# Row sums of attention: all four heads added at once on GpSimd, one key block left to the ones-matmuls, and new durations in the scheduler's model

## The chip, the cores and the metric

The kernel runs on one core of a Trainium2 chip. The metric is the device time of one execution in microseconds; lower is better. The engines are named as the profile names them: PE (TensorE, matmuls; PEld are its weight loads), DVE (VectorE), ACT (ScalarE), POOL (GpSimd) and SP (SyncE, whose queue issues the DMAs here).

## The reference

One transformer block on x of shape (2, 1024, 512): a modulated layer norm, causal attention with 32 query heads over 8 key/value heads of width 64 and rotary positions, a gated residual, a second modulated layer norm, and a feed-forward block with ternary weights. The part that matters here is attention's softmax:

```python
scores = jnp.einsum('bhqd,bhkd->bhqk', q, k) / jnp.sqrt(jnp.float32(D))
scores = jnp.where(causal[None, None], scores, jnp.finfo(x.dtype).min)
attn = jax.nn.softmax(scores, axis=-1)
out = jnp.einsum('bhqk,bhkd->bhqd', attn, v)
return out.transpose(0, 2, 1, 3).reshape(b, s, H * D) @ Wo
```

All of it is fp32. Every output row is divided by the sum of its exponentials over the keys: the row sum.

## The kernel before, in words

**Stages.** First come layer norm, the projections to q, k and v and the rotation (to about 340 us), written out in a fixed order. Then attention (about 340 to 1400 us) and the feed-forward (to the end), both put in order by a planner. The quantization of the feed-forward's weights (`ternary`, line 1074, 48 pieces) runs inside the attention stage.

**Units.** Attention works in 64 units (line 511): a batch, a group of four query heads that share a key head, and a block of 256 queries (i = 0 to 3). A unit has `nb = 2 * i + 2` key blocks of 128 keys: 2, 4, 6 or 8, in 16 units each. The last two blocks lie on the diagonal; in the very last one only 128 of the 256 queries count.

**Steps of a unit.** Before the scores, PE multiplies q with k once to get each row's maximum (`pm`); DVE reduces these from PSUM (`mx`), joins them (`mm`, line 771), and PE, ACT and a DMA turn them into one more row of the q tile, so that the scores come out with the maximum subtracted. For each key block j: two score matmul pairs (`score`, two heads each) into PSUM; two ACT exponentials (`expo`) into the tile `e` (four heads by 256 queries; 5 buffers); on the last two blocks a POOL select that zeroes the future (`causal`, line 827); and the value matmuls (`value`, line 833) in full fp32, which accumulate into `po`. The exponentials are also added over the key blocks into the tile `acc` (`total`, line 846): per block POOL adds heads 0 and 1 in one instruction and head 2 in another, DVE adds head 3. With two blocks only, ACT copies the half that has one addend (`first_total`). At the end of a unit four matmuls with a tile of ones, 32 columns wide, sum `acc` over the partitions, one head each, side by side in the array (`row_sum`, line 902). The result goes by ACT and DMAs through DRAM, is inverted, comes back as `ri`, and DVE multiplies the output with it (`normalize`); ACT and DVE split the product in a high and a low part, and six matmuls for each half project it (`project`), after which DVE adds it to the output rows `oacc`.

**What sets the order.** Every step is a task (`add`, line 70) with an engine, an assumed cost in us, a due time, the tasks it waits for, and the buffers it takes. `Plan.run` (line 90) plays the tasks through at these costs: each time it takes the engine that can start first, and there, among the tasks that could start, the one with the earliest due time, with an advance of 4 us for tasks of PE's present mode. Mode 1 is full fp32 (`value`, `row_sum`), mode 0 all the rest. The order in which tasks are taken is the program order of each engine; on the chip every engine works strictly in it and waits by semaphore. The costs come from small formulas: `pe`, `dv`, `po`, `ac` (lines 523 to 533). They decide the order only. PSUM has 3 score buffers, 4 buffers shared by `pm`, `pr`, `pj`, `pq` and others, and one for `po`. The queue of an engine is therefore a list fixed in advance; what is late in it holds all that stands behind it.

Of the kernel before, what the change touches and what calls it, by code (L numbers as in the profile page):

```python
# [58 lines left out]
class Plan:  # L59
# [30 lines left out]
    def run(self):  # L90
        wait, then, ready = {}, {}, {}
        for t in self.tasks:
            deps = {d.n: d for d in t.after + t.before}
            wait[t.n] = len(deps)
            for d in deps.values():
                then.setdefault(d.n, []).append(t)
            if not deps:
                ready.setdefault(t.eng, []).append((0.0, t))
        free, moving, ring, modes, left = {}, 0.0, 0.0, {}, len(self.tasks)
        while left:  # L100
            best = None
            for eng, ts in ready.items():
                opts = []
                for r, t in ts:
                    at = self.room(t)
                    if at is not None:
                        opts.append((max(r, at), t))
                if not opts:
                    continue
                start = max(free.get(eng, 0.0), min(o[0] for o in opts))  # L110
                if best is not None and start >= best[0]:
                    continue
                t = min((o for o in opts if o[0] <= start), key=lambda o: (o[1].due - STICK * (o[1].mode == modes.get(eng)), o[1].n))[1]
                best = (start, t)
            start, t = best
            left -= 1
            ready[t.eng] = [o for o in ready[t.eng] if o[1] is not t]
            for tag in t.takes:
                self.slots[self.alias.get(tag, tag)].append(lambda t=t, tag=tag: t.users[tag])
            t.emit()  # L120
            if t.eng == "T" and t.mode < modes.get("T", 0):
                start += 0.09
            modes[t.eng] = t.mode
            free[t.eng] = t.done = start + t.cost
            if t.eng is None:
                free[None] = t.done = 0.0
            if t.dma:
                ring = max(start + (0.26 if t.eng == "A" else 0.03), ring) + t.cost
                free[t.eng] = ring
                moving = max(ring + 0.7, moving) + t.dma / 360e3  # L130
                t.done = moving + 0.95
            for d in then.get(t.n, ()):
                wait[d.n] -= 1
                if not wait[d.n]:
                    r = max([a.done + (self.LAG if a.eng != d.eng or a.dma else 0.1) for a in d.after], default=0.0)
                    ready.setdefault(d.eng, []).append((r, d))
# [7 lines left out]
def block_kernel(ctx, tc, x, wq, wk, wv, wo, wgu, wpj, cin, wmod, cos, sin, out):  # L144
# [378 lines left out]
    def pe(n):  # L523
        return n / 2400 + 0.003

    def dv(n):
        return 0.069 + n / 960

    def po(n):
        return 0.05 + n * 0.0023  # L530

    def ac(n, psum=True):
        return (0.05 if psum else 0.094) + n / 1200

    KB = 1024
    add = plan.add
# [136 lines left out]
    def attention(u):  # L673
# [18 lines left out]
        if i == 0:  # L692
# [46 lines left out]
            lw = add("S", 0.46, t0 - 2, load_wo, order=(opened,), takes=("wos",), dma=512 * KB)  # L739
            wh = [add("A", ac(512, 0), t0 + 5 + 2 * c, lambda c=c: wo_hi(c), (lw,), takes=(("woH",), ())[c]) for c in range(2)]  # L740
            wh[1].order(wh[0])
            wl = [add("V", dv(512), t0 + 6 + 3 * c, lambda c=c: wo_lo(c), (wh[c],), takes=(("woL",), ())[c]) for c in range(2)]
            wl[1].order(wl[0])
            lw.hold("wos", *wh, *wl)
            wd["t"] = wh + wl
# [48 lines left out]
        for n, a in enumerate(jobs):  # L794
# [4 lines left out]
            m.hold("x", r)  # L799
            tops.append(m)  # L800
            reds.append(r)
        jn = add("V", 0.077, t0 - LEAD, top_join, reds, takes=("mm",))
        z.hold("mx", jn)
        tt = add("T", 0.11, t0 - LEAD, top_T, (jn,), takes=("x",))
        jn.hold("mm", tt)
# [37 lines left out]
            d["on"] = tp.tile([128, 512], F32, name="on", bufs=4)  # L843
            A.activation(d["on"].rearrange("p (a q) -> p a q", q=256), d["po"], AF.Copy)

        def total(j, eng, hs):
            q0 = 128 if j == nb - 1 else 0
            if "acc" not in d:
                d["acc"] = gp.tile([128, 4, 256], F32, name="acc", bufs=3)
            a = d["e", 0] if j == 1 else d["acc"]  # L850
            eng.tensor_tensor(d["acc"][:, hs, q0:], a[:, hs, q0:], d["e", j][:, hs, q0:], ALU.add)

        def first_total():
            d["acc"] = gp.tile([128, 4, 256], F32, name="acc", bufs=3)
            A.activation(d["acc"][:, :, 0:128], d["e", 0][:, :, 0:128], AF.Copy)

        ex, es, vals, sums, own = {}, {}, [], {}, None
        for j in range(nb):
            n = 128 if j == nb - 1 else 256
            due = due_s[(u, j)]  # L860
            es[j] = []
            for hp_ in range(2):
                p = add("T", 2 * pe(2 * n), due + 0.5 * hp_, lambda j=j, h=hp_: score(j, h),
                        [row, d["lq"][1], kd["one"]] + kd["l"] + d["lq"], takes=("s",))
                kd["use"].append(p)
                d.setdefault("sc", []).append(p)
                x_ = add("A", ac(2 * n), due + 0.5 + 0.5 * hp_, lambda j=j, h=hp_: expo(j, h), (p,), order=es[j],
                         takes=("e",) if hp_ == 0 else ())
                p.hold("s", x_)
                es[j].append(x_)  # L870
            ex[j] = es[j]
            if j >= nb - 2:
                ex[j] = [add("P", po(4 * 128) - 0.6, due - 1, lambda j=j: causal(j), es[j])]
            v = add("T", 2 * 4 * pe(n) + 0.05, due + 5, lambda j=j: value(j), ex[j] + [kd["lv"]], order=vals[-1:],
                    takes=("o",) if j == 0 else (), mode=1)
            kd["av"].append(v)
            vals.append(v)
            if j == 1 and nb == 2:
                own = add("A", ac(512, 0), due + 5, first_total, ex[0], order=(opened,), takes=("acc",))
            if j > 0:  # L880
                before = [own] if nb == 2 else sums[j - 1] if j > 1 else []
                q = []
                for a, z_ in ((0, 2), (2, 3)):
                    q.append(add("P", po((z_ - a) * n), due + 6, lambda j=j, a=a, z=z_: total(j, P, slice(a, z)), ex[j] + ex[0] + before,
                                 order=q[:1] or (opened,), takes=("acc",) if j == 1 and nb > 2 and not q else ()))
                if j == 1 and nb > 2:
                    own = q[0]
                q.append(add("V", dv(n), due + 6, lambda j=j: total(j, V, slice(3, 4)), ex[j] + ex[0] + before, order=(q[0],)))
                sums[j] = q
        for j in range(nb):  # L890
            users = [vals[j]] + (sums[j] if j else sums[1])
            if j == 0 and nb == 2:
                users.append(own)
            es[j][0].hold("e", *users)
        d["lq"][0].hold("t1", *tops, *d["sc"])
        d["lq"][1].hold("t2", *d["sc"])
        kd["use"].extend(tops)
# [3 lines left out]

        def row_sum():
            d["pr"] = xtile([128, 256], "pr")
            for h in range(4):
                T.matmul(d["pr"][h * 32:h * 32 + 32, :], ones, d["acc"][:, h, :], start=True, stop=True)

        def row_copy():
            d["ls"] = tp.tile([128, 256], F32, name="ls", bufs=1)
# [14 lines left out]
            for a in range(2):  # L923
                SY.dma_start(d["ri"][a * 64:a * 64 + 64, :], linv[u][a:a + 1, :].broadcast_to([64, 512]))

        rs = add("T", 4 * pe(256) + 0.15, t1_ + 4, row_sum, sums[nb - 1] + (sums[nb - 2] if nb > 2 else [own]), takes=("x*",), mode=1)
        own.hold("acc", rs)
        rc = add("A", ac(256), t1_ + 5, row_copy, (rs,), takes=("ls",))
        rs.hold("x*", rc)
        rt = add("S", 0.63, t1_ + 5, row_turn, (rc,), takes=("l8",), dma=16 * KB)  # L930
# [28 lines left out]
            else:  # L959
                V.tensor_tensor(acc, acc, d["pj", s], ALU.add)  # L960

        nm = add("V", dv(512), t1_ + 13, normalize, (gi, out_))
        gi.hold("ri", nm)
        hi_ = add("A", ac(512, 0), t1_ + 15, high, (nm,), takes=("oH",))
        lo_ = add("V", dv(512), t1_ + 17, low, (hi_,), takes=("oL",))
        out_.hold("on", hi_, lo_)
        pj = [add("T", 6 * pe(512), t1_ + 19 + s, lambda s=s: project(s), [hi_, lo_] + wd["t"], takes=("x*",)) for s in range(2)]
        hi_.hold("oH", *pj)
# [3 lines left out]
        for s in range(2):  # L972
# [1 line left out]
            sm.append(add(*(("A", ac(512)) if g == 0 else ("V", dv(512))), t1_ + 20 + s, lambda s=s: sum_up(s), [pj[s]] + prev_add.get(key, [])))  # L974
            pj[s].hold("x*", sm[s])
            prev_add[key] = [sm[s]]
        left_users.extend(tops + d["sc"] + vals + reds + [jn, tt, tc_, row] + sums[nb - 1] + sums[1] + ([own] if nb == 2 else []))
        outer_users.extend(())
        tail_users.extend(pj + sm + [pi, rt, nm])
        if i == NI - 1:  # L980
# [59 lines left out]
        lr = add("S", 0.46, t2_ - 10, load_r, order=(opened,), takes=("xr",), dma=512 * KB)  # L1040
        st_ = []
        for s in range(2):
            g_ = add("V", dv(512), t2_ + 3 * s, lambda s=s: gate(s), (sm[s], gated))
            r_ = add("V", dv(512), t2_ + 1 + 3 * s, lambda s=s: resid(s), (g_, lr))
            st_.append(add("V", dv(512) + 0.2, t2_ + 2 + 3 * s, lambda s=s: stat(s), [r_] + st_, takes=("sm",) if s == 0 else ()))
        va = add("V", 0.07, t2_ + 6, var, st_)
        ro = add("P", 0.65, t2_ + 6, root, (va,))
        nr = [add("V", 0.46, t2_ + 7 + s, lambda s=s: norm2(s), (ro,)) for s in range(2)]
        st_[0].hold("sm", *nr)
        turns, puts = [], []  # L1050
        his, los = [], []
# [22 lines left out]
    def ternary(n, src, dst, due):  # L1074
# [53 lines left out]
        p = add("T", pe(512), due + 9, group, (z,), takes=("x*",))  # L1128
        s_ = add("V", dv(512), due + 10, scale, (p,), takes=("ws",))
        p.hold("x*", s_)  # L1130
        k = add("V", dv(512), due + 11, pick, (s_,), takes=("wm_",))
        f = add("V", dv(256), due + 12, diff, (k,))
        v = add("V", dv(256), due + 13, back, (f,))
        m = add("V", dv(256), due + 14, masked, (v,))
        z.hold("wabs", p, v, k)
        k.hold("wm_", m)
        o = add("P", po(512), due + 15, signed, (m, g), takes=("wr",))
# [292 lines left out]
```

## Time and profile before

| | |
|---|---|
| median of 3 runs | 1769.24 us (1767.22 to 1771.09) |
| the profiled execution's own time | 1768.19 us |
| its span in the profile | 1766.5 us |
| mean granted PE clock | 0.977 |
| PE, DVE, ACT, POOL busy, share of the span | 94%, 78%, 41%, 58% |
| POOL adds into `acc`, first adds and others | 127.1 and 392.9 us in 512 instructions |
| DVE adds into `acc` | 178.7 us in 256 instructions |
| ones-matmuls `pr` | 46.4 us busy |
| causal selects on POOL | 128, 749 ns each |

The profile gives, for one execution, the busy time of each engine, groups of instructions with the mean duration of one and the idle time in front of them, who ended each wait, and the chain of work that ended last. A full-fp32 matmul appears as two records, and a matmul's end is modelled; the distance from one start to the next is the better measure of what it costs PE.

### The profile page before, as it was taken

How to read it: one execution, taken by the hardware profiler on the slowest of the kernel's cores; microseconds unless marked ns; L12 is line 12 of the kernel's file. 1: busy time of each engine (PE TensorE's matmuls, PEld its weight loads, DVE VectorE, ACT ScalarE, POOL GpSimd, SP SyncE). 2: the span in 40 equal slices, each digit the busy share in tenths (PEclk: the TensorE clock that was granted, in tenths of full speed). 3: DMA queues.
4: the chain of work that ended last, by engine and by line, in shares of the span. 5: the costliest groups of instructions: out<-in, count | busy, mean ns of one | idle time of the engine just before them, and what ended most of it. 6: DMA issues, size and time to landing. Idle time of an engine off the chain costs nothing.

```text
span 1766.5 us, 24175 instructions
## 1 busy us (share of the span) xinstructions
PE 1664.9 (94%) x7716; PEld 1124.3 (64%) x7716; DVE 1384.5 (78%) x2790; ACT 732.5 (41%) x1413; POOL 1029.0 (58%) x1060
## 2 busy tenths in 40 slices
PE   9899997799999989999999999999999999999998
PEld 7778885555555555555555555555555687888886
DVE  6778882789899989989999989889898854535354
ACT  3222220365555546545455546555554422222221
POOL 3445452576667666766666766666665844444343
PEclk9999998899999999999989999999999999999999
DMA  8785779754535534534435545534424643010000
GB/s 251 199 212 114 202 173 227 197 176 119 125 91 155 127 96 121 133 84 121 115 120 132 150 121 151 132 109 112 124 65 138 223 160 119 25 48 25 1 24 24
DMA packets 183032, 222.60 MB, mean 126 GB/s; under 512 B 30324, under 2 KB 122996, under 8 KB 182904
## 3 DMA queue, kind: packets, MB, share of 16 engines
q1 hardware_dynamic: 182904, 221.05, 45.3%
q8 instruction: 61, 1.00, 0.2%
q14 instruction: 67, 0.55, 0.1%
HBM read 148.90 MB, written 71.57 MB: 125 GB/s over the span
## 4 chain that ended last, share of the span: by engine, by line
PE 54%; DVE 27%; DMA 8%; issue 7%; SPq 2%; ACT 1%; POOL 1%; DVEq 0%; ACTq 0%; POOLq 0%
PE pgu L39 12%; PE pqk L39 8%; PE po L39 7%; PE pfo L39 7%; PE pj L39 6%; PE pm L39 4%; DVE acc L39 4%; DVE junk L39 4%; DVE oacc L39 3%; DVE ws L39 3%; DVE mx L39 2%; DMA ri<-linv 2%; SPq L39 2%; DMA linv<-l 2%; DVE on L39 1%
## 5 line engine op out<-in xcount | busy, mean ns | idle before, releaser
L39 POOL TENSOR_TENSOR acc<-acc,e 128x256 f32<-128x256 f32 (+2 forms) x384 | 392.9, 1044 | 46.1 <-ACT e L39 42.3
L39 PE MATMUL po<-e,vt 128*64 128x512 f32 (+1 forms) x1280 | 291.6, 568 | 5.1 <-POOL e L39 5.1
L39 DVE CUSTOM_DVE_ANT_0 junk<-pm,cmask 128x512 bf16<-128x512 f32 (+3 forms) x512 | 261.9, 548 | 36.3 <-PE pm L39 35.8
L39 PE MATMUL pm<-k,t 128*128 128x384 f32 (+3 forms) x768 | 247.2, 374 | 44.6 <-DVE mx L39 36.2
L39 PE MATMUL pgu<-h,gu 128*128 128x512 f32 x1024 | 248.1, 394 | 0.7 <-ACT gs L39 0.7
L39 PEld LDWEIGHTS pm<-k,t 128*128 128x128 f32 x768 | 140.7, 193 | 137.2 <-DVE mx L39 71.4
L39 PEld LDWEIGHTS pgu<-h,gu 128*128 128x128 f32 x1024 | 191.4, 188 | 46.2 <-issue 1.7
L39 POOL TENSOR_SCALAR_AFFINE_SELECT e<-e 128x512 f32<-128x512 f32 x128 | 95.3, 749 | 129.2 <-ACT e L39 114.0
L39 POOL TENSOR_TENSOR s<-hm 128x512 f32<-128x512 f32 x59 | 62.8, 1065 | 174.8 <-DVE hm L39 168.0
L39 PEld LDWEIGHTS po<-e,vt 128*64 128x64 f32 x1280 | 75.2, 136 | 138.1 <-issue 108.6
L39 POOL TENSOR_TENSOR acc<-e 128x256 f32<-128x256 f32 (+2 forms) x128 | 127.1, 1010 | 60.5 <-ACT e L39 55.8
L39 DVE TENSOR_TENSOR mL<-hm,mH 128x512 fp32r<-128x512 f32 x64 | 84.4, 1319 | 82.1 <-ACT mH L39 82.1
L39 DVE TENSOR_TENSOR acc<-acc,e 128x256 f32<-128x256 f32 x192 | 131.7, 686 | 9.3 <-POOL e L39 6.4
L39 DVE TENSOR_REDUCE mx<-pm 128x1 f32<-128x384 f32 (+2 forms) x256 | 130.6, 545 | 5.3 <-PE pm L39 4.9
L39 DVE TENSOR_TENSOR hm<-gs,pgu 128x512 f32<-128x512 f32 x64 | 43.9, 686 | 106.2 <-PE pgu L39 106.2
L39 POOL TENSOR_TENSOR wr<-ws,wsg 128x512 fp32r<-128x512 bf16 x48 | 61.4, 1279 | 96.4 <-DVE ws L39 79.6
L39 ACT ACTIVATE mH<-hm 128x512 fp32r<-128x512 f32 x64 | 40.4, 632 | 169.2 <-PE pfo L39 145.6
L39 POOL TENSOR_TENSOR ra<-ra,rb 128x512 f32<-128x512 f32 x40 | 51.8, 1294 | 99.1 <-DVE rb L39 89.0
L39 PE MATMUL pfo<-pj,mH 128*128 128x512 f32 x256 | 101.2, 395 | 0.0
L39 PE MATMUL pfo<-pj,mL 128*128 128x512 f32 x256 | 100.3, 392 | 0.0
L39 PE MATMUL pj<-woH,oH 128*128 128x512 f32 x256 | 86.4, 419 | 6.3 <-DVE mx L39 3.3
L39 DVE TENSOR_TENSOR oacc<-oacc,pj 128x512 f32<-128x512 f32 x112 | 75.4, 676 | 15.7 <-PE pj L39 15.2
(2152 smaller groups left out, 3564.4 us busy)
## 6 DMA issues: line engine op xcount, KB each, us to landing
qs<-rr SPq DMA_DIRECT2D x128, 256.0 KB
t<-qs SPq DMA_DIRECT2D x64, 512.0 KB
t<-qs SPq DMA_DIRECT2D x64, 256.0 KB
ri<-linv SPq DMA_DIRECT2D x128, 128.0 KB
k<-ks SPq DMA_DIRECT2D x48, 256.0 KB
ks<-rr SPq DMA_DIRECT2D x32, 256.0 KB
wos<-in_wo SPq DMA_DIRECT2D x16, 512.0 KB
w<-in_wgu SPq DMA_DIRECT2D x32, 256.0 KB
```

Of the source, the lines that this page charges most:

```text
L39: ins = f(*a, **k)
```

## The change

Three things. (1) `total` becomes one POOL instruction for all four heads of a block, 1,024 columns; DVE adds nothing any more, and ACT's copy is gone. (2) The block before the last (`nb - 2`) is not added: `row_sum` takes it straight from its `e` tile with four ones-matmuls of 256 columns, and four more on `acc` accumulate onto them. With two blocks nothing is added at all: four ones-matmuls run on block 0 and four of 128 columns on block 1. The `e` tile of such a block is held until the row sum. (3) The planner's model gets other durations: a new formula `dd` for DVE operations with two SBUF inputs, higher values for POOL, ACT and some small operations, and a price for each change of PE's mode, 0.1 us into fp32 and 0.2 us out of it, where a change out of fp32 cost 0.09 us.

```diff
-            if t.eng == "T" and t.mode < modes.get("T", 0):
-                start += 0.09
+            if t.eng == "T" and t.mode != modes.get("T", 0):
+                start += 0.1 if t.mode else 0.2
...
+    def dd(n):
+        return 0.1 + n * 0.0015
     def po(n):
-        return 0.05 + n * 0.0023
+        return 0.2 + n * 0.0021
     def ac(n, psum=True):
-        return (0.05 if psum else 0.094) + n / 1200
+        return (0.075 if psum else 0.1) + n / 1200
...
-        jn = add("V", 0.077, t0 - LEAD, top_join, reds, takes=("mm",))
+        jn = add("V", 0.35, t0 - LEAD, top_join, reds, takes=("mm",))
...
-        def total(j, eng, hs):
+        def total(j):
             q0 = 128 if j == nb - 1 else 0
-            if "acc" not in d:
+            if j == 1:
                 d["acc"] = gp.tile([128, 4, 256], F32, name="acc", bufs=3)
             a = d["e", 0] if j == 1 else d["acc"]
-            eng.tensor_tensor(d["acc"][:, hs, q0:], a[:, hs, q0:], d["e", j][:, hs, q0:], ALU.add)
-
-        def first_total():
-            d["acc"] = gp.tile([128, 4, 256], F32, name="acc", bufs=3)
-            A.activation(d["acc"][:, :, 0:128], d["e", 0][:, :, 0:128], AF.Copy)
+            P.tensor_tensor(d["acc"][:, :, q0:], a[:, :, q0:], d["e", j][:, :, q0:], ALU.add)
...
-                ex[j] = [add("P", po(4 * 128) - 0.6, due - 1, lambda j=j: causal(j), es[j])]
+                ex[j] = [add("P", 0.68, due - 1, lambda j=j: causal(j), es[j])]
...
-                for a, z_ in ((0, 2), (2, 3)):
-                    q.append(add("P", po((z_ - a) * n), due + 6, lambda j=j, a=a, z=z_: total(j, P, slice(a, z)), ex[j] + ex[0] + before,
-                                 order=q[:1] or (opened,), takes=("acc",) if j == 1 and nb > 2 and not q else ()))
...
-                q.append(add("V", dv(n), due + 6, lambda j=j: total(j, V, slice(3, 4)), ex[j] + ex[0] + before, order=(q[0],)))
+            if nb > 2 and j > 0 and j != nb - 2:
+                adds[j] = add("P", po(4 * n), due + 6, lambda j=j: total(j), ex[j] + (ex[0] if j == 1 else sums[-1:]),
+                              order=(opened,), takes=("acc",) if j == 1 else ())
+                sums.append(adds[j])
...
         def row_sum():
             d["pr"] = xtile([128, 256], "pr")
-            for h in range(4):
-                T.matmul(d["pr"][h * 32:h * 32 + 32, :], ones, d["acc"][:, h, :], start=True, stop=True)
+            for n, (a, q0) in enumerate(((d["e", nb - 2], 0), (d["acc"], 0) if nb > 2 else (d["e", 1], 128))):
+                for h in range(4):
+                    T.matmul(d["pr"][h * 32:h * 32 + 32, q0:], ones, a[:, h, q0:], start=(n == 0), stop=(n == 1))
...
-        rs = add("T", 4 * pe(256) + 0.15, t1_ + 4, row_sum, sums[nb - 1] + (sums[nb - 2] if nb > 2 else [own]), takes=("x*",), mode=1)
-        own.hold("acc", rs)
+        rs = add("T", 8 * pe(256 if nb > 2 else 192) + 0.15, t1_ + 4, row_sum, sums[-1:] + ex[nb - 2] + ex[nb - 1], takes=("x*",), mode=1)
+        if sums:
+            sums[0].hold("acc", rs)
+        for j in range(nb):
+            users = [vals[j]]
+            if nb == 2 or j == nb - 2:
+                users.append(rs)
+            else:
+                users.append(adds[j or 1])
+            es[j][0].hold("e", *users)
...
-        nm = add("V", dv(512), t1_ + 13, normalize, (gi, out_))
+        nm = add("V", dd(512), t1_ + 13, normalize, (gi, out_))
...
-        lo_ = add("V", dv(512), t1_ + 17, low, (hi_,), takes=("oL",))
+        lo_ = add("V", dd(512), t1_ + 17, low, (hi_,), takes=("oL",))
```

The other edits of the third kind, not shown, put `dd` in place of `dv` for the low part of wo, the gate and residual and one step of `ternary`, 0.45 us for three more of its steps, and 0.7 for 0.46 us for the second layer norm.

More of the change, by code (lines that the diff above doesn't have):

```diff
@@ L741, in attention @@
             wh[1].order(wh[0])
-            wl = [add("V", dv(512), t0 + 6 + 3 * c, lambda c=c: wo_lo(c), (wh[c],), takes=(("woL",), ())[c]) for c in range(2)]
+            wl = [add("V", dd(512), t0 + 6 + 3 * c, lambda c=c: wo_lo(c), (wh[c],), takes=(("woL",), ())[c]) for c in range(2)]
             wl[1].order(wl[0])
@@ L844, in copy_out @@
             A.activation(d["on"].rearrange("p (a q) -> p a q", q=256), d["po"], AF.Copy)
-        def total(j, eng, hs):
+        def total(j):
             q0 = 128 if j == nb - 1 else 0
-            if "acc" not in d:
+            if j == 1:
                 d["acc"] = gp.tile([128, 4, 256], F32, name="acc", bufs=3)
             a = d["e", 0] if j == 1 else d["acc"]
-            eng.tensor_tensor(d["acc"][:, hs, q0:], a[:, hs, q0:], d["e", j][:, hs, q0:], ALU.add)
-        def first_total():
-            d["acc"] = gp.tile([128, 4, 256], F32, name="acc", bufs=3)
-            A.activation(d["acc"][:, :, 0:128], d["e", 0][:, :, 0:128], AF.Copy)
-        ex, es, vals, sums, own = {}, {}, [], {}, None
+            P.tensor_tensor(d["acc"][:, :, q0:], a[:, :, q0:], d["e", j][:, :, q0:], ALU.add)
+        ex, es, vals, sums = {}, {}, [], []
+        adds = {}
         for j in range(nb):
@@ L877, in attention @@
             vals.append(v)
[L878 to L882, printed above, removed]
-                for a, z_ in ((0, 2), (2, 3)):
-                    q.append(add("P", po((z_ - a) * n), due + 6, lambda j=j, a=a, z=z_: total(j, P, slice(a, z)), ex[j] + ex[0] + before,
-                                 order=q[:1] or (opened,), takes=("acc",) if j == 1 and nb > 2 and not q else ()))
-                if j == 1 and nb > 2:
-                    own = q[0]
-                q.append(add("V", dv(n), due + 6, lambda j=j: total(j, V, slice(3, 4)), ex[j] + ex[0] + before, order=(q[0],)))
[L889 to L894, printed above, removed]
+            if nb > 2 and j > 0 and j != nb - 2:
+                adds[j] = add("P", po(4 * n), due + 6, lambda j=j: total(j), ex[j] + (ex[0] if j == 1 else sums[-1:]),
+                              order=(opened,), takes=("acc",) if j == 1 else ())
+                sums.append(adds[j])
         d["lq"][0].hold("t1", *tops, *d["sc"])
@@ L976, in attention @@
             prev_add[key] = [sm[s]]
-        left_users.extend(tops + d["sc"] + vals + reds + [jn, tt, tc_, row] + sums[nb - 1] + sums[1] + ([own] if nb == 2 else []))
+        left_users.extend(tops + d["sc"] + vals + reds + [jn, tt, tc_, row] + sums + [rs])
         outer_users.extend(())
@@ L1042, in attention @@
         for s in range(2):
-            g_ = add("V", dv(512), t2_ + 3 * s, lambda s=s: gate(s), (sm[s], gated))
-            r_ = add("V", dv(512), t2_ + 1 + 3 * s, lambda s=s: resid(s), (g_, lr))
+            g_ = add("V", dd(512), t2_ + 3 * s, lambda s=s: gate(s), (sm[s], gated))
+            r_ = add("V", dd(512), t2_ + 1 + 3 * s, lambda s=s: resid(s), (g_, lr))
             st_.append(add("V", dv(512) + 0.2, t2_ + 2 + 3 * s, lambda s=s: stat(s), [r_] + st_, takes=("sm",) if s == 0 else ()))
@@ L1047, in attention @@
         ro = add("P", 0.65, t2_ + 6, root, (va,))
-        nr = [add("V", 0.46, t2_ + 7 + s, lambda s=s: norm2(s), (ro,)) for s in range(2)]
+        nr = [add("V", 0.7, t2_ + 7 + s, lambda s=s: norm2(s), (ro,)) for s in range(2)]
         st_[0].hold("sm", *nr)
@@ L1130, in ternary @@
         p.hold("x*", s_)
[L1131 to L1134, printed above, removed]
+        k = add("V", dd(512), due + 11, pick, (s_,), takes=("wm_",))
+        f = add("V", 0.45, due + 12, diff, (k,))
+        v = add("V", 0.45, due + 13, back, (f,))
+        m = add("V", 0.45, due + 14, masked, (v,))
         z.hold("wabs", p, v, k)
```

## The prediction

> **What bounds the kernel now.** I read the shares of busy time first, then the table by stretches of time, to learn which stage has room. A stretch's columns are its length, busy time with count of PE, PEld, DVE, ACT and POOL, the granted PE clock, the DMA share and GB/s:
>
> ```profile
> PE 1664.9 (94%) x7716; PEld 1124.3 (64%) x7716; DVE 1384.5 (78%) x2790; ACT 732.5 (41%) x1413; POOL 1029.0 (58%) x1060
> ...
> 200.00:300.00 100.00, 96.13 (x431) 78.82 (x429) 70.82 (x94) 19.18 (x34) 49.02 (x39) 1.00 0.80 184
> ...
> 900.00:1000.00 100.00, 90.32 (x427) 52.72 (x425) 94.74 (x222) 54.41 (x108) 71.83 (x76) 0.97 0.46 132
> ...
> 1500.00:1600.00 100.00, 100.00 (x440) 81.70 (x439) 49.94 (x54) 24.95 (x43) 42.45 (x36) 1.00 0.12 42
> ```
>
> The projections (to 340 us) and the feed-forward (from 1400 us) are PE's own work and the change does not touch them. In attention, about 340 to 1400 us, DVE is as full as PE. So the question is who waits for whom there. The chain of waits between 700 and 1000 us shows one such place, and PE's timeline beside it:
>
> ```profile
> 904.75 3.27 DVE oacc L39 x4
> 908.02 1.42 DVE acc L39
> 909.45 1.73 DVE xr L39 x2
> 911.43 0.58 PE pq L39
> ```
>
> ```profile
> 908.56 0.22 PE L39 MATMUL pm<-k,t 128*128 128x128 f32 x1
> 911.43 0.58 PE L39 MATMUL pq<-wabs,gones 128*128 128x512 bf16 x1 [2.65 <-DVE mx L39]
> ```
>
> PE stands idle for 2.65 us because no PSUM buffer is free: the maxima that would free one are queued on DVE, and one thing in front of them is a row-sum add of 1.42 us. The waits between 420 and 1380 us say how much of this there is (total, times, longest):
>
> ```profile
> PEld pm L39 <- DVE mx L39: 45.5, 73, 2.8
> PEld pmT L39 <- DVE mm L39: 25.5, 23, 2.5
> PE pm L39 <- DVE mx L39: 15.0, 19, 2.3
> PEld po L39 <- POOL e L39: 7.1, 13, 1.6
> ```
>
> DVE leads by far; POOL is small. PE and PEld rows overlap, so I made the sum from PE's start times in 340 to 1400 us (1,060 us): each matmul at its usual start-to-start (0.23 us for 512 fp32r columns, 0.43 us for each of the two passes of an fp32 group of 512) gives 875 us of work; a change between fp32r and fp32 adds 0.1 us, 329 times, 31 us; start-up excesses under 0.13 us, nearly all without a releaser, 51 us; real waits 102 us, of which DVE 72 (mx 39, mm 13, oacc 8, acc 5, rest small), ACT 11, POOL 6, no releaser 12. So 72 us is the most that relief of DVE can give, before what PE gets to carry.
>
> **The change, part by part.** The rows for the adds (idle time before them after the bar):
>
> ```profile
> L39 POOL TENSOR_TENSOR acc<-acc,e 128x512 f32<-128x512 f32 x144 | 204.7, 1421 | 36.8 <-ACT e L39 34.2 <-DMA ri<-linv 1.1
> L39 POOL TENSOR_TENSOR acc<-acc,e 128x256 f32<-128x256 f32 x192 | 169.2, 882 | 9.2 <-ACT e L39 8.1
> L39 DVE TENSOR_TENSOR acc<-acc,e 128x256 f32<-128x256 f32 x144 | 104.6, 726 | 7.4 <-POOL e L39 4.6 <-ACT e L39 2.2
> L39 DVE TENSOR_TENSOR acc<-acc,e 128x128 f32<-128x128 f32 x48 | 27.1, 565 | 1.9 <-POOL e L39 1.8
> L39 PE MATMUL pr<-acc,ones 128*32 128x256 f32 x512 | 46.4, 405 | 4.9 <-DVE acc L39 1.8 <-DVE mx L39 1.7 <-POOL acc L39 0.9
> ```
>
> *DVE loses its adds.* 144 and 48 of these and the first adds (48 x 812 ns, 16 x 498 ns): 104.6 + 27.1 + 39.0 + 8.0 = 179 us. In attention DVE falls from about 91% to about 74%. The Trainium skill speaks against such a move: GPSIMD Engine Reference, "Performance versus the Vector engine", gives 2,293 ns for a DVE add of 2,048 fp32 and 4,497 ns on GpSimd, so elementwise work belongs on DVE. By that price the adds would weigh 192 x 0.29 + 64 x 0.14 = 64 us on DVE; it would fall only to 85%, and I would then let DVE's waits drop by about the 25 us that PE gains in work: no change, 1768. The row says 726 ns for 256 columns, 2.5 times the page's price, beside a busy POOL. The row counts: 179 us.
>
> *POOL.* It now has 192 adds for 512. The slope of its rows is (1421 - 882)/256 = 2.1 ns a column, so 1,024 columns cost 1.42 + 512 x 0.0021 = 2.50 us (the page's rate gives 2.25; both ends stay). 144 x 2.50 + 48 x 1.4 = 427 us, against 393 + 127 = 520 before: 93 us less, since the same columns go in fewer instructions. It had a third of its time free, so this is worth nothing by itself. But one add now holds POOL for up to 2.5 us, and behind it in the queue stand causal selects (749 ns), which the last two value matmuls of each unit wait for.
>
> *PE gets more ones-matmuls.* 64 units issue 8 instead of 4; four heads run side by side. In the chain, `po` groups of x4 take 1.01 us and x8 1.87, so one more fp32 group of 512 columns costs 0.86 us and one of 256 costs 0.43. 48 units get one of 256 (20.6 us), 16 units one of 128 (3.4 us): +24 us, all on the path, since nothing on PE hides PE. The instruction order as built has 346 changes between fp32 and fp32r for 334: +1.2 us. The row sum's own waits are no later than before: it waits for the selects, which the value matmuls in front of it have already waited for, and for the last add on POOL; behind it on PE stand the next unit's scores and maxima. The cost cannot be below this: the upper end is a further 0.1 us for each group started late, 6 us.
>
> *ACT* loses 16 copies of 630 ns, 10 us on an engine half busy: nothing; if it were not covered, at most its 11 us of PE waits would shrink.
>
> *Exponential tiles.* The unadded block is held until the row sum instead of until its add, and where there are only two blocks both are. Five tiles exist; scores wait if they run out. The trace has no such wait for scores on tiles held by a row sum. Bounds: -2 us (the chain of adds before the row sum is shorter) to +10 us; I take 0, because the row sum comes directly behind the unit's last value matmuls in the new order.
>
> *The new durations* change no instruction, only the order. They move towards the rows: join 0.077 to 0.35 (row 534 ns), normalize and low 0.60 to 0.87 (952 and 909), POOL 512 columns 1.23 to 1.28 (1421). The order before charged a DVE head 0.34 us where the row has 0.73, so DVE ran behind its order all through attention. Bounds from -15 us to +15 us; taken at 0 beyond what the DVE relief gives. The long wait of 19.9 us at 296 us, behind stores of q, is reached by the same instructions in the same order, and stays.
>
> *What is late next.* Of DVE's 72 us, acc's 5 go for certain. The rest is queueing for PSUM buffers and the maxima; with DVE at 74% for 91% the free share is almost three times as large (26% for 9%), so I estimate a third remains: 25 us. POOL's waits rise from 6 to about 8. Then: 1768.2 (this execution's own time) + 24 + 1.2 - 47 + 2 = 1748. The median of the runs is 1769.2, one us above the profiled one, which is inside their spread; no correction.
>
> **The rivals.**
> 1. *DVE's waits go almost wholly,* with the cold spells of the clock (0.97 in the row above) that follow PE's idle times: -65 - 5 + 25 = -45: 1723. For it: waits come in clusters, late maxima making later ones late. Against: maxima cost 0.55 to 0.68 us where their matmul takes 0.18 to 0.23, so bursts remain.
> 2. *The gain isn't there.* The waits are such bursts, four buffers deep, and a freer DVE does not shorten them: -5 (acc) - 12 (part of mm, oacc) + 25 = +8: 1776. Against: DVE at 95% in the stretch with the lowest PE share.
> 3. *POOL becomes the bound of the masked blocks (slower).* Place: the 128 causal selects and the value matmuls behind them. In the built orders, weighed with the measured durations, a quarter of the half-width value matmuls have under 2.75 us of PE work between their last score and themselves, for 3.95 before. Exponentials, select and handovers need about 1.8 us; an add of 2.5 us ahead breaks that. If half of the selects come 1 us late, PE waits 64 us: 25 - 47 + 64 = +42: 1810; a quarter gives +10: 1778. It decides once PE's waits for POOL exceed about 28 us. Against: POOL is a third idle, and the add of one block starts a whole block before the next select.
>
> **How the numbers follow.** The likeliest case 0.52 (1738 to 1758), first rival 0.15 (1715 to 1735), second 0.16 (1764 to 1782), third 0.17 (1770 to 1810). The range 1724 to 1784 leaves the outer half of the first rival and of the third out, about 0.16. A measurement of this kernel can tell 0.2%, 3.5 us. Faster by more: 0.52 + 0.15 + a little of the second, 0.67; within: 0.08; slower: 0.25.
>
> **What would show it.** Right: DVE near 74% in the attention stretches; PE waits on DVE mx, mm and oacc down to a third; `pr` busy roughly twice 46 us less the overlap; POOL adds of 1,024 columns at 2.3 to 2.6 us. Wrong: PE's waits for POOL's selects above 28 us in total; DVE waits still above 45 us at 74% load; PE waiting for scores because ACT waits for exponential tiles.

## The result, and the profile after

The changed kernel takes 1780.2 us (median of 4 runs, 1777.1 to 1780.8) against 1768.8 us for the kernel before beside it: ratio 1.006, interval 1.0042 to 1.0077. It is slower, where the forecast was 1748. Later runs of the kernel before, beside the experiments, have medians of 1770.4 to 1772.1, so the loss is 8 to 11 us.

The page's busy times and one stretch of the changed kernel:

```profile
PE 1675.0 (94%) x8218; PEld 1139.3 (64%) x8228; DVE 1320.4 (74%) x2534; ACT 717.6 (40%) x1397; POOL 933.0 (52%) x740
```

```profile
900.00:1000.00 100.00, 91.83 (x464) 54.85 (x464) 89.74 (x200) 53.40 (x108) 64.37 (x50) 0.97 0.48 133
```

256 adds of 178.7 us have left DVE, but its busy time fell by 64 us only. In the nine stretches from 400 to 1300 us it is at 85% on average, after 91%; the forecast had 74%. The waits between 420 and 1380 us show PE as before behind DVE:

```profile
PEld pmT L39 <- DVE mm L39: 32.9, 28, 3.0
PEld pm L39 <- DVE mx L39: 31.6, 51, 2.1
...
PE pmT L39 <- DVE mm L39: 15.6, 22, 2.1
...
PE pm L39 <- DVE mx L39: 11.0, 14, 1.7
...
PEld po L39 <- POOL e L39: 5.9, 16, 0.9
```

The waits for the reductions mx fell, those for the join mm rose, and POOL's selects (`po <- POOL e`) stayed small. The groups say where DVE's time went. First the changed kernel:

```profile
L39 POOL TENSOR_TENSOR acc<-acc,e 128x1024 f32<-128x1024 f32 x96 | 235.3, 2451 | 106.2 <-ACT e L39 102.8
...
L39 DVE TENSOR_TENSOR on<-on,ri 128x512 f32<-128x512 f32 x64 | 78.5, 1227 | 24.8 <-DMA ri<-linv 24.1 <-ACT wsg L39 0.6
L39 DVE TENSOR_TENSOR oacc<-oacc,pj 128x512 f32<-128x512 f32 x112 | 75.7, 681 | 57.2 <-PE pj L39 57.2
L39 DVE TENSOR_TENSOR oL<-on,oH 128x512 fp32r<-128x512 f32 x64 | 75.1, 1173 | 4.3 <-ACT oH L39 4.2
...
L39 DVE TENSOR_TENSOR mm<-mx 128x8 f32<-128x8 f32 x64 | 59.9, 936 | 0.3
```

and the same groups of the kernel before:

```profile
L39 DVE TENSOR_TENSOR oacc<-oacc,pj 128x512 f32<-128x512 f32 x112 | 75.4, 676 | 15.7 <-PE pj L39 15.2
L39 DVE TENSOR_TENSOR on<-on,ri 128x512 f32<-128x512 f32 x64 | 60.9, 952 | 17.4 <-DMA ri<-linv 17.4
L39 DVE TENSOR_TENSOR oL<-on,oH 128x512 fp32r<-128x512 f32 x64 | 58.1, 909 | 2.0 <-ACT oH L39 1.6
...
L39 DVE TENSOR_TENSOR mm<-mx 128x8 f32<-128x8 f32 x64 | 34.2, 534 | 0.3
```

None of these DVE instructions was edited. The three with two SBUF inputs (`on`, `oL`, `mm`) became longer by 29 to 75%; `oacc`, with one input in PSUM, did not. The join handles 8 columns and takes 936 ns, though the shortest of its kind takes 150. The timeline of the changed kernel shows what it does in that time:

```profile
822.15 5.15 POOL L39 TENSOR_TENSOR acc<-acc,e 128x1024 f32<-128x1024 f32 x2 [4.82 <-ACT e L39]
823.28 1.78 DVE L39 TENSOR_TENSOR oL<-on,oH 128x512 fp32r<-128x512 f32 x1
824.99 2.33 DVE L39 TENSOR_TENSOR mm<-mx 128x8 f32<-128x8 f32 x1
...
827.38 0.27 PE L39 MATMUL pmT<-ident,mm 128*8 128x128 f32 x1 [0.90 <-DVE mm L39]
```

The two POOL adds end at 827.30 (822.15 + 5.15), the join at 827.32. It waited for the second add to end, counted as busy all the while. This is no single case: 20 of the 64 joins take under 180 ns, and every one of the other 44 ends 17 to 35 ns after the end of a POOL instruction. In the kernel before the same holds for 36 of the 64 (18 to 29 ns). It works the other way too: of the 144 POOL adds of 1,024 columns, the 35 that began while such a DVE instruction was running take 2.64 us on average (up to 2.93), the other 109 take 2.38 (up to 2.54).

So theory A: **a DVE instruction with two SBUF inputs waits until the POOL instruction under way has ended.** What it waits (a hold, below) grows with the length of POOL's instructions, and the change replaced 512 adds of 0.5 to 1.4 us by 192 of 1.4 to 2.45. I added up, from the score matmuls on to 1430 us, how much each DVE instruction takes beyond the shortest of its kind: 257 us before, 90 of them in the adds themselves; 257 us after, without them. (Some 45 us of each sum are the small spread of instructions that never wait.) As much waiting as left with the adds came back in the others. That the two sums are equal is chance: in another order the same instructions give 230 (e8_old_durations below).

Two inputs are not the whole of it. This DVE instruction of the changed kernel has one SBUF input and waits too:

```profile
1379.26 2.39 POOL L39 TENSOR_TENSOR acc<-e 128x1024 f32<-128x1024 f32 x1 [1.32 <-ACT e L39]
1379.35 2.33 DVE L39 TENSOR_SCALAR ve<-mv 128x2 f32<-128x2 f32 x1
```

It adds a constant to two columns, 160 ns when nothing is in its way, and ends 27 ns after the POOL add. Of the eight of its kind from 850 us on, five are held like this one.

Theory B: PE's added ones-matmuls explain the result, and the holds of DVE delay no other engine. Theory C: the new durations spoilt the order.

### The profile page after: what moved, and what is told of

Its sections match the earlier page's. It is cut to its first block, busy times and chain, and to the rows that moved or that the text cites. A ratio compares the mean times of both kernels' runs of the same rounds, so it can differ in the third digit from the quotient of the medians.

```text
span 1778.0 us, 24351 instructions
## 1 busy us (share of the span) xinstructions
PE 1675.0 (94%) x8218; PEld 1139.3 (64%) x8228; DVE 1320.4 (74%) x2534; ACT 717.6 (40%) x1397; POOL 933.0 (52%) x740
## 4 chain that ended last, share of the span: by engine, by line
PE 45%; DVE 17%; issue 4%; DMA 4%; ACT 1%; SPq 0%; POOL 0%; DVEq 0%; ACTq 0%; POOLq 0%
PE pgu L39 12%; PE po L39 7%; PE pfo L39 6%; PE pj L39 6%; PE pm L39 4%; DVE junk L39 3%; DVE ws L39 2%; DVE oL L39 2%; DVE oacc L39 2%; DVE mx L39 2%; PE pr L39 2%; DMA ri<-linv 2%; DVE mm L39 2%; DVE on L39 2%; DMA l<-ls 1%
## 5 line engine op out<-in xcount | busy, mean ns | idle before, releaser
L39 POOL TENSOR_TENSOR acc<-acc,e 128x512 f32<-128x512 f32 (+1 forms) x144 | 302.8, 2103 | 109.6 <-ACT e L39 102.8
L39 DVE CUSTOM_DVE_ANT_0 junk<-pm,cmask 128x512 bf16<-128x512 f32 (+3 forms) x512 | 262.5, 549 | 45.5 <-PE pm L39 44.4
L39 PE MATMUL pm<-k,t 128*128 128x384 f32 (+3 forms) x768 | 232.7, 366 | 32.9 <-DVE mx L39 30.9
L39 POOL TENSOR_TENSOR acc<-e 128x1024 f32<-128x1024 f32 x48 | 116.4, 2424 | 143.5 <-ACT e L39 143.5
L39 DVE TENSOR_TENSOR on<-on,ri 128x512 f32<-128x512 f32 x64 | 78.5, 1227 | 24.8 <-DMA ri<-linv 24.1
```

What stands on the lines that cost most here:

```text
L39: ins = f(*a, **k)
```

## The experiments

Each of the following differs from the changed kernel, or from the one before where it says so, by the lines shown or by the part of the change that is named.

**e1_split2: the add in two instructions.**

```diff
-            P.tensor_tensor(d["acc"][:, :, q0:], a[:, :, q0:], d["e", j][:, :, q0:], ALU.add)
+            for n in range(0, 4, 2):
+                hs = slice(n, n + 2)
+                P.tensor_tensor(d["acc"][:, hs, q0:], a[:, hs, q0:], d["e", j][:, hs, q0:], ALU.add)
```

> The changed kernel, with each GpSimd add given as two instructions of two heads (512 columns) in the same place of the order; all else stays. Theory A (an add on POOL holds a DVE instruction with two SBUF inputs until the add ends, so the longer adds gave DVE's relief back to its other instructions): the join mm goes from 941 ns to about 650, normalize and low from 1.2 us to about 1.0, PE's waits in the attention stage from 98 to about 88 us, the time from 1780 to 1769 to 1775. Theory B (PE's 24 us of added ones-matmuls explain everything, the holds reach nobody): 1777 to 1783. Theory C (the new durations spoilt the order): the order is the same, so 1777 to 1783 too.

1744.7 us, ratio to before 0.9847 (0.9819 to 0.9875); the changed kernel had 1.006. The direction is theory A's; the effect, 35 us, is more than three times the most that I had expected (11). PE's work is unchanged, so B can't make it; nor can C, with the order the same on every engine. The rows of this kernel:

```profile
L39 DVE TENSOR_TENSOR on<-on,ri 128x512 f32<-128x512 f32 x64 | 61.1, 954 | 34.6 <-DMA ri<-linv 33.4 <-ACT wsg L39 1.0 <-ACT e L39 0.2
...
L39 DVE TENSOR_TENSOR mm<-mx 128x8 f32<-128x8 f32 x64 | 40.3, 629 | 0.3
```

The join is down from 936 (the row above; the expectation has 941) to 629 ns, and the time beyond the shortest from 257 to 201 us. POOL itself is busier, 984.5 us for 933.0: the length of one instruction counted, not POOL's load.

**e2_join: the join with one SBUF input.**

```diff
-            V.tensor_tensor(d["mm"], d["mx"][:, :, 0], d["mx"][:, :, 1], ALU.max)
+            V.tensor_reduce(d["mm"], d["mx"], AX.X, ALU.max)
```

> The changed kernel, with the join of the maxima as a reduction over one SBUF tensor instead of a maximum of two SBUF inputs; order and result stay. Theory A: the join takes under 250 ns whatever POOL does, where it took 941; PE's waits for mm go from 21 to under 8 us, the time to 1766 to 1774. Theory B: the join is short too, but others take its place and the time stays at 1776 to 1782. If a reduction from SBUF is held as well, the join stays at 0.9 us and theory A is wrong about two inputs.

1772.3 us (22 runs, 1765.5 to 1781.5), 8 us less than the changed kernel, which was not run beside it; ratio to before 1.0004 (0.9986 to 1.0021), where the changed kernel had 1.006. The row:

```profile
L39 DVE TENSOR_REDUCE mm<-mx 128x8 f32<-128x16 f32 x64 | 10.3, 161 | 0.3
```

161 ns on average, though 45 of the 64 begin beside a POOL instruction. This reduction is never held. It shows that the form of the instruction matters, not that one SBUF input is enough: `ve` above has one as well. PE's waits for mm fell from 20.7 to 4.3 us; as theory B said, some of the others rose (mx 34 to 38, oL 4 to 6), but not all of it was taken.

**e3_small_adds: the adds cut short.** Each add takes 8 columns for each head, and the row sum takes the unadded block twice: the adds are in effect left out, and the row sums are other ones.

```diff
-            P.tensor_tensor(d["acc"][:, :, q0:], a[:, :, q0:], d["e", j][:, :, q0:], ALU.add)
+            P.tensor_tensor(d["acc"][:, :, 0:8], a[:, :, 0:8], d["e", j][:, :, q0:q0 + 8], ALU.add)
...
-            for n, (a, q0) in enumerate(((d["e", nb - 2], 0), (d["acc"], 0) if nb > 2 else (d["e", 1], 128))):
+            for n, (a, q0) in enumerate(((d["e", nb - 2], 0), (d["e", nb - 2], 0) if nb > 2 else (d["e", 1], 128))):
```

> The changed kernel with the adds cut to 8 columns for each head (the row sum takes the unadded block twice, so the adds are in effect left out and the row sums are other ones), with PE's work, the waits and the order kept. Theory A: with POOL nearly free of adds DVE's time beyond the shortest of each kind falls from 257 us to under 130 and PE's waits from 98 to about 60 us: 1735 to 1752. Theory B: at most the few us in which PE waited for POOL are gone: 1772 to 1780.

1711.2 us, ratio 0.9659 (0.9631 to 0.9686), 69 us below the changed kernel and more than theory A had said. The join takes 212 ns, the time beyond the shortest is 101 us, and PE waits 27 us in the stage. One stretch of this kernel beside the one above:

```profile
900.00:1000.00 100.00, 99.97 (x548) 60.51 (x545) 78.04 (x208) 57.33 (x117) 28.55 (x54) 1.00 0.59 157
```

In this stretch PE is all but without a gap, at full clock, and DVE at 78%. This is the picture that the prediction had drawn for the change. It needs POOL nearly free of adds.

**e4_new_durations: the kernel before, with the third part of the change alone** (and `dd(n)` as the price of DVE's adds).

> The kernel before with the new durations and mode prices alone (DVE's share of the adds at the new two-input price). Theory C: slower than before by about 10 us, 1776 to 1784. Theories A and B: the order is no worse, 1760 to 1772.

1772.3 us against 1772.1, ratio 0.9997 (0.9979 to 1.0015): no difference. Theory C falls for the kernel before.

**e8_old_durations: the changed kernel, with the third part undone.**

> The changed kernel (adds of four heads unsplit) with the durations and mode prices of before. Theory C (the new durations cost something with the new adds): 1764 to 1773. Theory A: the holds are the same, 1775 to 1785.

1796.8 us, ratio to before 1.0157 (1.0129 to 1.0185). Both theories missed: the first two parts of the change, long adds and added ones-matmuls together, cost 26 us, and the new durations bring back 17 of them. In the stage PE waits 38 us for mm here, 21 in the changed kernel.

**e5_split4: the add in four instructions** (`range(0, 4)`, one head each).

> The changed kernel, with each add given as four instructions of one head (256 columns), in the same place of the order. The two-head split gave 1744.7. Theory A (a DVE instruction with two SBUF inputs waits until the running POOL add ends): the longest wait is now about 0.7 us, DVE's time beyond the shortest of each kind falls from 201 to about 150 us, PE's waits from 61 to about 48, 1732 to 1742; POOL itself works about 40 us longer in all, off the path. If the count of POOL's instructions matters more than their length, each giving DVE's instruction one more wait: 1744 to 1755.

1733.8 us, ratio 0.9794 (0.9773 to 0.9814), as theory A had it. The time beyond the shortest is 173 us, more than the 150 expected; POOL is busy 1,060 us, 127 more than in the changed kernel. PE pays little for that: between 420 and 1380 us its matmuls wait 3.3 us for POOL's selects, after 0.7, and their weight loads 10.0, after 5.9.

**e6_all_added_split2: PE's added work taken away instead.** The block before the last is added too, on POOL, in two instructions; where there are more than two blocks PE has four ones-matmuls again. Their cost in the planner, the release of the `e` tile and a flag of the matmul follow and are not shown; the order is another one, too.

```diff
-            if nb > 2 and j > 0 and j != nb - 2:
+            if nb > 2 and j > 0:
...
-            for n, (a, q0) in enumerate(((d["e", nb - 2], 0), (d["acc"], 0) if nb > 2 else (d["e", 1], 128))):
+            for n, (a, q0) in enumerate([(d["e", 0], 0), (d["e", 1], 128)] if nb == 2 else [(d["acc"], 0)]):
```

> The changed kernel with adds split in two, and the block before the last added as well where there are more than two blocks, so that PE has four ones-matmuls there for eight: 20 us less of PE's work, 48 more pairs of POOL adds (about 130 us of POOL). PE's work on the path at full price with no holds: 1744.7 - 20 = 1725. Theory A: the longer busy POOL holds DVE more often (excess from 201 to about 235 us) and PE waits some 15 us more: 1738 to 1748.

1760.6 us (12 runs, 1754.2 to 1770.4), 16 us more than e1_split2 although PE's work is 20.6 us less. PE's waits went from 61 to 93 us, twice the rise that theory A had put; half of it, 17 us, is for DVE, whose time beyond the shortest rose by 36 us. The rest is not taken apart; PE's weight loads for the ones-matmuls now also wait 9.3 us for POOL's last add. So the unadded block is worth its 20 us of PE here, in part by the holds that it saves.

**e7_split2_join and e9_split4_join: both remedies.**

> The changed kernel with adds split in two and the join as a reduction over one SBUF tensor. The join alone gave 8 us on the unsplit kernel. Theory A: its hold, 30 us in all here, goes; PE waits for mm 6.7 us now, so 1736 to 1744. A rival to that: with DVE relieved the join isn't on the path any more, 1743 to 1747.

> The changed kernel with adds in four instructions of one head and the join as a one-input reduction. Theory A: the join's remaining hold (24 us in all, of which PE waits for 2.6) goes: 1727 to 1733 after 1733.8 with the split alone. If nothing is left to win on this path: 1732 to 1736.

1735.9 us (ratio 0.9807, 0.9783 to 0.9831) and 1730.3 us (0.9769, 0.9738 to 0.98). The first gains 9 us over the split in two, just past the better end of theory A's range (1732.9 to 1741.4 after 1743.8 to 1746.0, not run side by side). The second is 3.5 us under the split in four with ranges that overlap (1724.5 to 1736.5 and 1732.0 to 1735.2): that step is not settled. Of the versions that compute the whole block it is the fastest, 40 us under the kernel before.

**e10_before_single: the kernel before, with its two-head adds in two instructions.**

```diff
-            eng.tensor_tensor(d["acc"][:, hs, q0:], a[:, hs, q0:], d["e", j][:, hs, q0:], ALU.add)
+            for h in range(hs.start, hs.stop):
+                eng.tensor_tensor(d["acc"][:, h, q0:], a[:, h, q0:], d["e", j][:, h, q0:], ALU.add)
```

> The kernel before with its two-head POOL adds given as two instructions of one head each; DVE's share, the order and PE's work stay. Theory A says that the kernel before paid for holds as well: DVE's time beyond the shortest of each kind falls from 257 to about 215 us and the time by 5 to 12 us: 1758 to 1766. If the holds only matter with instructions above 2 us: 1768 to 1774.

1743.9 us, ratio 0.9842 (0.9816 to 0.9868). The kernel before paid for holds as well, 26 us of its time at least, twice the upper end of what I expected. The time beyond the shortest is 222 us, near the 215 expected. This is also the fairer partner for e5_split4: with all adds of 256 columns at most in both, the three parts of the change together gain 10 us (1743.9 to 1733.8).

**e11_old_durations_split4: short adds with the old durations.**

> The changed kernel's adds in four instructions of one head, with the durations and mode prices of before. The new durations were worth 17 us with the long adds (1796.8 to 1780.2) and nothing on the kernel before. If they help by placing DVE's instructions around long holds, little is left of it: 1735 to 1743. If they give a better order in itself for the new adds: 1746 to 1755.

1737.7 us, ratio 0.9801 (0.9773 to 0.9829): of the 17 us that the new durations brought with long adds 4 are left, and the runs of the two overlap (1732.0 to 1741.3 and 1732.0 to 1735.2). That fits durations that helped mostly by working around the holds, as I had expected for that case.

The stage from the first score matmul to the 193rd feed-forward matmul, in one profile each (PE's work, its changes between fp32 and fp32r, and its waits, by the method of the prediction; "DVE beyond shortest" is the sum explained above, to 1430 us; the last column is the time at half clock; all in us):

| kernel | stage | PE work | changes | waits | of them DVE | DVE beyond shortest | half clock |
|---|---|---|---|---|---|---|---|
| before | 1130.8 | 941.2 | 31.4 | 104.2 | 73.2 | 257 | 37.5 |
| changed | 1145.7 | 965.3 | 32.7 | 95.5 | 65.7 | 257 | 34.1 |
| e1_split2 | 1108.2 | 965.3 | 32.2 | 60.9 | 35.3 | 201 | 23.9 |
| e5_split4 | 1098.3 | 965.3 | 32.1 | 51.0 | 23.8 | 173 | 17.1 |
| e3_small_adds | 1071.6 | 965.3 | 32.0 | 26.7 | 11.6 | 101 | 6.8 |
| e6_all_added_split2 | 1121.2 | 944.7 | 33.1 | 93.4 | 51.9 | 237 | 34.1 |
| e8_old_durations | 1165.4 | 965.3 | 27.8 | 122.5 | 83.8 | 230 | 44.4 |

(The changed kernel's trace lacks 2.4 us of matmul records; its work is that of its twin programs and its waits are reduced by as much.) What work, changes and waits leave of the stage is 48 to 54 us in every row: the kernels differ by PE's waits.

## Why the prediction was wrong, point by point

**The step that failed** is "*DVE loses its adds* ... The row counts: 179 us" with what followed, DVE at 74% and a third of its 72 us of PE waits left: 47 us off the time. The instructions went, but DVE's busy time fell by 64 us only, to 85% in the stage, and PE's waits for DVE only from 73 to 66. I had the sign that a row of 726 ns for 256 columns was odd, 2.5 times what I had estimated from the price in the Trainium skill (GPSIMD Engine Reference, "Performance versus the Vector engine"), and read it as DVE's work. About half of it was waiting: the shortest of these adds took 361 ns, and 90 of the 179 us lay beyond the shortest. In the sums above such waits did not leave with the instructions that had them: the other DVE instructions of the kind took as much. The same page's "Specifications" call GpSimd's SBUF interfaces shared with VectorE, with "contention with DVE instructions in a 2-port perf mode or with two SBUF inputs"; this case's trace gives it its size: until POOL's instruction ends. Whether the one-input `ve` ran in such a mode, no run here shows.

I also costed POOL's longer instruction only for what stands behind it in POOL's own queue. Its price was on another engine: the same adds in four instructions each take 46 us off the time.

**What held.** PE's ones-matmuls: +24 us forecast, 27.5 to 51.5 us in the stage. The changes of mode: +1.2 forecast, +1.3. POOL's adds: 427 us forecast, 144 at 2.44 us and 48 at 1.41, 419 us. In the stage the sum is 24.1 + 1.3 - 8.7 (waits) and 2 us less of small gaps: 14.9 us; the profile's stage began 3.6 us earlier, which leaves the 11 us of the result. (It began anywhere from 327.5 to 333.5 us in the profiles of the table; the change does not touch what stands ahead of it.)

**What I took at zero.** The new durations: nothing on the kernel before, -17 us with the long adds, just beyond my bound of 15. They hid part of the miss: with the old ones the changed kernel takes 1796.8 us, and what I had put at 21 us of gain is a loss of 26. The exponential tiles: no wait of scores for a row sum shows among PE's larger waits.

**The rivals.** The third, selects late behind long adds, didn't come: PE waits 2.2 us for them in the stage. The second, 1776 us, was next to the result for a wrong reason: the waits weren't bursts of reductions, since they went with the length of POOL's instructions. The first, 1723, is nearest to what the change does once its adds are short, 1733.8, but only 10 us of that are the change's own; splitting the kernel before's adds gave the rest.

**Not settled.** Why 58 us less of DVE's busy time from the changed kernel to e1_split2 took 35 us off PE's waits, and 64 us less from the kernel before to the changed one only 9, is argued and not shown: the holds of the changed kernel are fewer and longer, up to 2.3 us, and a long one uses up what the order has in hand. Nor is it settled how much of each gain is the clock's: half-clock spells in the stage fall with PE's waits, from 34 us to 24 with the split in two. They come after idle time: in the profile of the kernel before, from 335 to 1470 us, the 3.4 us ahead of a half-clock window of 3.4 us hold 1.4 us of idle PE on average, ahead of the others 0.1.

## What to carry to other kernels

Before you take a DVE row for work, look at the spread of its durations: a long mean over a short minimum, on an instruction with two SBUF inputs, can be waiting for GpSimd; it is, when the long ones end just behind a GpSimd instruction. Where both engines work side by side, try short GpSimd instructions, even at the price of more of them, and give DVE's short critical steps a form that the trace shows unheld, here a reduction over one SBUF tensor. One SBUF input alone is no guarantee.

## What the runs showed of the hardware that I had not expected

Short instructions don't always let DVE in. In e5_split4 nine POOL adds ran back to back, and a join that began during the second waited for the end of the ninth:

```profile
1278.58 6.20 POOL L39 TENSOR_TENSOR acc<-acc,e 128x256 f32<-128x256 f32 x9
1279.16 0.55 DVE L39 CUSTOM_DVE_ANT_0 junk<-pm,cmask 128x384 bf16<-128x384 f32 x1
1279.63 0.08 DVE L39 DVE_READ_ACCUMULATOR2_ANT mx<- 128x1 f32 x1
1279.63 5.18 DVE L39 TENSOR_TENSOR mm<-mx 128x8 f32<-128x8 f32 x1
```

5.18 us for 8 columns; the reduction just before it, which reads PSUM and one SBUF tile, was not delayed. A normalize in the same run took 3.99 us in the same way. It is no accident of one profile: all three kernels that give POOL the four heads one by one have such holds, one normalize of 3.98 us in e9_split4_join and three of 3.16 to 5.04 us in e11_old_durations_split4, each across five to seven POOL instructions, while no DVE instruction of the other ten profiles took longer than 2.92 us. Most held joins of e5_split4, 41 of 47, still got in at the end of one POOL instruction; what decides it stays open.
